# Multiplying dt u with B for two state steps in one VectorE instruction: a Mamba, GPTQ, attention and mixture sandwich on one core

## The chip, the cores and the metric

The kernel runs on one core of a Trainium2 chip. The metric is the device time of one execution in microseconds (us); three runs of the kernel before gave 953.85, 954.11 and 956.48, with a median of 954.11.

## The reference

Four layers, each `x = x + layernorm(layer(layernorm(x)))`, on x of 2 batches x 512 tokens x 512 channels, all in float32. The first layer is a Mamba block with 1024 inner channels and 16 states, the second a feed-forward layer with 4-bit weights that are unpacked first, the third an attention of one key head, the fourth a mixture of a shared feed-forward layer and a latent one. The change concerns the recurrence of the first, which runs over the tokens:

```python
def step(state, inp):
    dt_t, B_t, C_t, u_t = inp
    dA = jnp.exp(dt_t[..., None] * A)
    state = state * dA + (dt_t * u_t)[..., None] * B_t[:, None, :]
    y = jnp.einsum('bdn,bn->bd', state, C_t)
    return (state, y)
...
y = ys.transpose(1, 0, 2) + x * D
y = y * jax.nn.silu(gate)
return y @ W_out.T
```

## The kernel before

The inner channels lie on the 128 partitions, in 8 chunks, and the 512 tokens on the free axis. A "step" of the kernel is one batch, one chunk and two of the 16 states (NG = 2): 2 x 8 x 8 = 128 steps, numbered s; `k, gi = divmod(s, 8)` gives the chunk k (0 to 15, the second batch from 8 on) and the pair of states gi. In a step

- ScalarE makes exp(dt A) for both states into one of two PSUM tiles (`exps`, line 1002), two steps ahead;
- VectorE multiplies du (dt times u, 128x512, in PSUM, made once a chunk on line 1016) with B of the two states, broadcast over the partitions, into a state buffer `bx` of 128x1024 (`times_B`, line 1018), one step ahead;
- VectorE runs the recurrence over the tokens in place in `bx` (`scan`, line 1022);
- GpSimd multiplies `bx` with C, in place (`times_C`, line 1028); in some steps of the second batch it also adds the two states (line 1030);
- TensorE adds the two states (or their sum) into y in PSUM by matmuls with the identity (`sums`, line 1050), two steps later; the first of a chunk adds D u (line 1045). The gate is multiplied with y on VectorE (`fin`, line 1056) at gi = 2 of the next chunk.

`bx` comes from a pool of six buffers of one tag. A product that takes a buffer anew waits for the sums of the step that had it.

B and C are 16 tiles of 128x1024 (512 KB when written), one each for every gi. `states` loads them from a scratch in DRAM, broadcast to 128 partitions, on SP's DMA queue, B and C alternately: all 16 of the first batch just ahead of the loop, those of the second batch one gi a step during the last chunk of the first (steps 56 to 63).

In between, TensorE works through a fixed stream of other matmuls (`stream`: gates, the second batch's input projections, W_out of the first batch, and most of the second layer's first feed-forward product), portioned so that sums and stream together make 3.5 us a step by the kernel's own estimate (STEP). Other engines get the parts of these as jobs, released by a clock that ticks twice a step. The instruction order of TensorE, ScalarE, VectorE and GpSimd is that of the program's text: `pin` chains them. The order of SP's queue is the scheduler's. W_out's tiles (line 862) share three buffers with the other weights.

The main loop in its order, cut to what the change touches:

```python
for s in range(NS + 3):
    ...
    tick()
    if gi == 4 and k + 1 < len(order):
        diag(k + 1)
    if 0 < s < NS - 1:
        times_B(s + 1)
        if gi == NGI - 2 and k + 1 < len(order):
            new_du(k + 1)
    tick()
    if s < NS:
        scan(s)
```

`new_du` is ScalarE's copy of the next chunk's dt into du. So the order on VectorE is product, scan, product, scan, with jobs between.

Of the kernel before, what the change touches and what calls it, by code (L numbers as in the profile page):

```python
# [9 lines left out]
F32 = mybir.dt.float32  # L10
# [8 lines left out]
P = 128  # L19
B = 2  # L20
S = 512
# [13 lines left out]
NG = 2  # L35
NGI = N_ST // NG
# [20 lines left out]
def tile_sandwich(  # L57
# [72 lines left out]
    def minus_mean(mv, rs, name, n=TB, beside_scan=False):  # L130
        if beside_scan:
            nm = stat.tile([P, TB], F32, tag="nm", name=f"nm_{name}")
            if n == 1:
                nc.gpsimd.tensor_scalar(nm[:, :1], mv[:, 0, 0:1], rs[:, 0:1], -1.0, ALU.mult, ALU.mult)
            else:
                nc.gpsimd.tensor_mul(nm[:, :n], mv[:, :n, 0], rs[:, :n])
                nc.gpsimd.tensor_scalar(nm[:, :n], nm[:, :n], -1.0, None, ALU.mult)
            return nm
        nm = stat.tile([P, TB], F32, tag="nm", name=f"nm_{name}")
        nc.vector.scalar_tensor_tensor(  # L140
            nm[:, :n], mv[:, :n, 0], -1.0, rs[:, :n], ALU.mult, ALU.mult
        )
        return nm
# [278 lines left out]
    with ExitStack() as mamba:  # L422
# [3 lines left out]
        bcp = pool(mamba, "bc")  # L426
# [23 lines left out]
        for b in range(B):  # L450
            t_ = smp.tile([R_DT + 1, S], F32, tag=f"dtT{b}", name=f"dtT{b}")
# [3 lines left out]
        nc.gpsimd.dma_start(out=wx, in_=W_x)  # L455
        Bbs = [[None] * NGI for _ in range(B)]
        Cbs = [[None] * NGI for _ in range(B)]
        st = {}

        def w_in(part, b, c):  # L460
# [19 lines left out]
        def diag(k):  # L480

            c = k % NCH
            t_ = dgp.tile([P, P], F32, tag="dg", name=f"dg{k}")
            nc.scalar.activation(t_, ident, AF.Copy, scale=ch[:, c, KCONV + 1 : KCONV + 2])
            st["diag", k] = t_
# [49 lines left out]
        def states(b, gi):  # L535

            for lst, lo, nm in ((Bbs[b], 0, "B"), (Cbs[b], R_C - R_B, "C")):
                t_ = bcp.tile([P, NG, S], F32, tag=f"{nm}{gi}", name=f"{nm}{b}_{gi}")
                n0 = lo + gi * NG
                ins = nc.sync.dma_start(  # L540
                    out=t_, in_=scr[b][n0 : n0 + NG, :].partition_broadcast(P)
                )
                lst[gi] = t_
            return ins

        def dt_in(b, c):
            ps = mbank(f"pv{b}_{c}")
            nc.tensor.matmul(ps, wdt[:, ts(c, P)], dtT[b], start=True, stop=True)
            return ps
# [9 lines left out]
        with ExitStack() as p1:  # L559
# [10 lines left out]
            for i in range(TB + 2):  # L570
# [4 lines left out]
                if 0 <= i - 1 < TB:  # L575
                    j = i - 1
                    rs = rn[j]
                    nm = minus_mean(mvs[j], rs, f"m0_{j}", 1)
# [59 lines left out]
            for gi in range(NGI):  # L638
                last = states(0, gi)
# [8 lines left out]
            return g1p.tile([P, cols], dt, tag=f"g1{i}", name=name)  # L648

        with ExitStack() as p2:  # L650
            bxp = pool(p2, "bx", 6)
            ps_y = pool(p2, "p2y", 1, PSUM)
            ps_du = pool(p2, "p2du", 1, PSUM)
            ps_da1 = pool(p2, "p2da1", 1, PSUM)
# [13 lines left out]
            def spawn(gen, lag=0):  # L668
                jobs.append([now[0] + lag, gen])

            def tick():
                now[0] += 1
                for job in list(jobs):
                    if job[0] <= now[0]:
                        try:
                            job[0] = now[0] + next(job[1])
                        except StopIteration:
                            jobs.remove(job)
# [13 lines left out]
            def bank_free():  # L692
                return len(turns) < 2 or turns[-2][1] is not None
# [300 lines left out]
            NS = len(order) * NGI  # L994
            bxs = {}

            def exps(s):
                k, gi = divmod(s, NGI)
                b, c = order[k]
                for i in range(NG):  # L1000
                    n = gi * NG + i
                    nc.scalar.activation(  # L1002
                        das[s % 2][:, i, 1:], st["dt", b, c][:, 1:], AF.Exp, scale=A[:, c, n : n + 1]
                    )

            def new_du(k):

                b, c = order[k]
                du = st["du"] = ps_du.tile([P, S], F32, tag="du", name=f"du{b}_{c}")
                nc.scalar.copy(du, st["dt", b, c])  # L1010

            def times_B(s):
                k, gi = divmod(s, NGI)
                b, c = order[k]
                if gi == 0:
                    nc.vector.tensor_mul(st["du"], u[b][c], st["du"])
                bx = bxs[s] = bxp.tile([P, NG, S], F32, tag="bx", name=f"bx{b}_{c}_{gi}")
                nc.vector.tensor_mul(bx, st["du"].unsqueeze(1).to_broadcast([P, NG, S]), Bbs[b][gi])  # L1018

            def scan(s):  # L1020
                flat = bxs[s].rearrange("p n t -> p (n t)")
                nc.vector.tensor_tensor_scan(  # L1022
                    flat, das[s % 2].rearrange("p n t -> p (n t)"), flat, 0.0, ALU.mult, ALU.add
                )
# [7 lines left out]
            def paired(s):  # L1032

                k, gi = divmod(s, NGI)

                return order[k][0] == 1 and (k - NCH not in (2, 3) and gi in (1, 5) or k - NCH < 2 and gi % 2 == 1)

            def sums(s):
                k, gi = divmod(s, NGI)
                b, c = order[k]  # L1040
                ns = 1 if paired(s) else NG
                cost = ns * MM
                if gi == 0:
                    y = st["y"] = ps_y.tile([P, S], F32, tag="y", name=f"py{b}_{c}")
                    nc.tensor.matmul(y, st["diag", k], u[b][c], start=True, stop=False)
                    cost += MM
                bx = bxs.pop(s)
                for i in range(ns):
                    last = gi == NGI - 1 and i == ns - 1
                    nc.tensor.matmul(st["y"], ident, bx[:, i, :], start=False, stop=last)  # L1050
                return cost

            def fin(k):

                b, c = order[k]
                nc.vector.tensor_mul(g[b][c], g[b][c], st["y"])
                st[f"fin{k}"] = now[0]

            def dt_job(k, ps):
                dt_out(*order[k], ps)  # L1060
                release(f"pv{k}")
                yield 1
# [5 lines left out]
            exps(0)  # L1068
            exps(1)
            times_B(0)  # L1070
            free, dt_due = 0.0, None
            for s in range(NS + 3):
                k, gi = divmod(s, NGI)
                free = min(free, MM) + STEP
                if gi == 1 and k + 1 < len(order):
                    dt_due = k + 1
                if gi == 2 and k:
                    fin(k - 1)
                for part in ((1, 0) if gi == 2 or 2 <= s < NS + 2 and paired(s - 2) else (0, 1)):
                    if part == 0:  # L1080
                        if 0 <= s - 2 < NS:
                            free -= sums(s - 2)
                    else:
                        while free > 0 and s < NS:
                            if dt_due and bank_free():
                                turns.append([f"pv{dt_due}", None])
                                spawn(dt_job(dt_due, dt_in(*order[dt_due])), 2)
                                free -= MM
                                dt_due = None
                            cost = next(pe, None)  # L1090
                            if cost is None:
                                break
                            free -= cost
                tick()
                if gi == 4 and k + 1 < len(order):
                    diag(k + 1)
                if 0 < s < NS - 1:
                    times_B(s + 1)
                    if gi == NGI - 2 and k + 1 < len(order):
                        new_du(k + 1)  # L1100
                tick()
                if s < NS:
                    scan(s)
                    if s == 0:
                        times_B(1)
                    if s + 2 < NS:
                        exps(s + 2)
                    times_C(s)
                    if order[k] == (0, NCH - 1):
                        states(1, gi)  # L1110
                pin()
# [6 lines left out]
        with ExitStack() as p3:  # L1118
# [9 lines left out]
            for j in range(NCH // 2):  # L1128
                w = wo_pair(1, 0, j)
                for e in range(2):  # L1130
                    c = 2 * j + e
# [13 lines left out]
            for i, m in enumerate(IC):  # L1145
                j, e = divmod(i, 2)
                if not e:
                    w = wst.tile([P, 2, H], F32, tag="w4", name=f"wd0_{j}")
                    n = len(IC[i : i + 2])
# [287 lines left out]
```

## Time and profile before

| | |
|---|---|
| runs, median (lowest to highest) | 954.11 us (953.85 to 956.48) |
| the profiled execution, its own time | 955.89 us |
| its span, first to last instruction | 954.1 us |
| mean granted clock of TensorE | 0.959 |
| busy: TensorE, VectorE, GpSimd, ScalarE | 862.3, 675.2, 484.0, 420.2 us |
| first and last scan start | 74.0 and 570.4 us |

The profile is one execution. Its span is 1.8 us shorter than the time of the same execution, since that has what lies around the first and the last instruction. Busy time of TensorE is modelled, because matmuls overlap; its idle time before an instruction, with the engine that ended it, says more. In a group's line the two numbers after the bar are busy time in us and the mean duration of one in ns; after the second bar stands the idle time of the engine just before such instructions. In a timeline the first number is the start, the second the duration, in us; in brackets stand the idle time and what ended it. Durations on VectorE overlap with the next instruction's start, so what an instruction takes from the queue is read from start to start.

### The profile page before, as it was taken

Reading aid. Unit: us, or ns where it says so; the run is one execution under the profiler, and the core shown is the slowest. Engines: PE = TensorE matmul, PEld = TensorE weight load, DVE = VectorE, ACT = ScalarE, POOL = GpSimd, SP = SyncE. Lnnn points to the kernel's source line nnn. Section 1 sums busy time; section 2 is a strip of 40 time slices with the busy share of each in tenths; the row PEclk is TensorE's granted clock in tenths of the full one; section 3 lists DMA queues with packets and bytes.
Section 4 is the critical chain, followed back from the end, with each engine's and each line's share of the span. In section 5 each row is a group of like instructions: output and inputs, shape, how many; then the busy total and the mean of one; then the engine's idle time right before and its main releaser. Section 6 shows DMA issues by size and latency. Waiting matters only on the chain.

```text
span 954.1 us, 7148 instructions
## 1 busy us (share of the span) xinstructions
PE 862.3 (90%) x2184; PEld 386.6 (41%) x2184; DVE 675.2 (71%) x783; ACT 420.2 (44%) x631; POOL 484.0 (51%) x351
## 2 busy tenths in 40 slices
PE   6977989779989899579999999998999998999994
PEld 3532434333534434234433444444544444445441
DVE  4968999999999998999999995535610034534225
ACT  3335775656666655476655640125320014322122
POOL 5665796777877777876877884440000000011002
PEclk9978999898999989889999999999999999998997
DMA  6439211010002854300111103455223221200101
GB/s 182 163 124 387 69 37 38 30 37 31 22 23 83 297 187 152 89 0 0 45 44 45 30 9 124 150 159 198 58 64 89 58 89 45 66 12 30 48 0 44
DMA packets 43816, 80.08 MB, mean 84 GB/s; under 512 B 7774, under 2 KB 20937, under 8 KB 43778
## 3 DMA queue, kind: packets, MB, share of 16 engines
q1 hardware_dynamic: 41506, 73.64, 23.6%
q0 software_dynamic: 1984, 5.47, 1.6%
q10 hardware_dynamic: 288, 0.52, 0.2%
q8 instruction: 17, 0.28, 0.1%
q14 instruction: 21, 0.17, 0.1%
HBM read 68.37 MB, written 11.24 MB: 83 GB/s over the span
## 4 chain that ended last, share of the span: by engine, by line
PE 46%; DVE 28%; issue 11%; POOL 5%; DMA 2%; ACT 1%; SPq 0%; DVEq 0%; POOLq 0%; ACTq 0%
DVE bx L1022 11%; DVE bx L1018 8%; PE pd L1365 6%; PE py L1050 5%; PE pup L1302 5%; PE fo L1155 4%; PE fu L367 3%; PE fo L1218 3%; POOL bx L1028 3%; PE fg L367 3%; PE fu L947 3%; PE fg L947 3%; PE po L1133 3%; PE po L916 2%; DVE u L475 2%
## 5 line engine op out<-in xcount | busy, mean ns | idle before, releaser
L1028 POOL TENSOR_TENSOR bx<-bx,C 128x1024 f32<-128x1024 f32 x128 | 302.0, 2360 | 115.3 <-DVE bx L1022 90.7
L1022 DVE TENSOR_TENSOR_SCAN bx<-da,bx 128x1024 f32<-128x1024 f32 x128 | 291.6, 2279 | 0.1
L1050 PE MATMUL py<-bx,ident 128*128 128x512 f32 x480 | 238.1, 626 | 35.6 <-POOL bx L1028 32.3
L1002 ACT ACTIVATE da<-dt,A 128x511 f32<-128x511 f32 x256 | 176.3, 691 | 161.6 <-DVE bx L1022 155.7
L1018 DVE TENSOR_TENSOR bx<-du,B 128x1024 f32<-128x1024 f32 x128 | 154.4, 1206 | 9.0 <-DMA B<-scr 5.1
L1050 PEld LDWEIGHTS py<-bx,ident 128*128 128x128 f32 x480 | 91.5, 198 | 164.1 <-issue 93.1
L1231 DVE TENSOR_TENSOR it<-it,fu 128x512 f32<-128x512 f32 (+1 forms) x11 | 7.6, 688 | 72.3 <-PE fu L367 72.3
L1302 PE MATMUL pup<-hT_l,wup 128*128 128x512 f32 x128 | 57.5, 604 | 0.0
L381 POOL TENSOR_TENSOR sd<-ve,half 128x4 f16<-128x4 f16 x2 | 2.1, 1045 | 109.0 <-DVE ve L379 109.0
L709 PE MATMUL pg<-xT,w_g 128*128 128x512 f32 x120 | 57.1, 604 | 0.0
L1365 PE MATMUL pd<-wdn,hid 128*128 128x512 f32 x128 | 55.3, 592 | 0.0
L127 POOL TENSOR_TENSOR rs_lo<-ve_lo,mhalf 128x1 f32<-128x1 f32 x8 | 5.5, 684 | 78.0 <-DVE ve_lo L125 78.0
L947 PE MATMUL fg<-hT_f,wg 128*128 128x512 f32 (+1 forms) x88 | 42.1, 597 | 0.0
L475 DVE SCALAR_TENSOR_TENSOR u<-px,ch,u 128x511 f32<-128x511 f32 (+2 forms) x48 | 35.8, 746 | 7.0 <-ACT u L468 5.9
L367 PE MATMUL fg<-hT_f,wg 128*128 128x512 f32 (+1 forms) x88 | 40.2, 593 | 0.7 <-ACT hT_f L171 0.7
L947 PE MATMUL fu<-hT_f,wu 128*128 128x512 f32 (+1 forms) x88 | 40.7, 592 | 0.0
L367 PE MATMUL fu<-hT_f,wu 128*128 128x512 f32 (+1 forms) x88 | 39.8, 593 | 0.0
L1218 PE MATMUL fo<-wd,it 128*128 128x512 f32 (+1 forms) x88 | 39.6, 592 | 0.0
L1155 PE MATMUL fo<-wd,it 128*128 128x512 f32 (+1 forms) x88 | 38.0, 593 | 1.6 <-DMA wd<-wd_d 1.6
L1365 PEld LDWEIGHTS pd<-wdn,hid 128*128 128x128 f32 x128 | 24.2, 190 | 30.7 <-issue 30.1
L1302 PEld LDWEIGHTS pup<-hT_l,wup 128*128 128x128 f32 x128 | 24.5, 195 | 28.8 <-issue 28.8
L1230 ACT ACTIVATE it<-fg 128x512 f32<-128x512 f32 (+1 forms) x11 | 6.6, 597 | 65.7 <-PE fg L367 65.7
(224 smaller groups left out, 1161.4 us busy)
## 6 DMA issues: line engine op xcount, KB each, us to landing
wo<-in_W_outT SPq DMA_DIRECT2D x20, 512.0 KB
B<-scr SPq DMA_DIRECT2D x16, 512.0 KB
C<-scr SPq DMA_DIRECT2D x16, 512.0 KB
wg<-wgu_d SPq DMA_DIRECT2D x10, 512.0 KB
wu<-wgu_d SPq DMA_DIRECT2D x10, 512.0 KB
w_x<-in_W_in SPq DMA_DIRECT2D x8, 512.0 KB
wgu_d<-w_gu POOLq DMA_DIRECT2D x16, 256.0 KB, 2.3
w_g<-in_W_in SPq DMA_DIRECT2D x8, 512.0 KB
```

What stands on the lines that cost most here:

```text
L367: nc.tensor.matmul(ps[:m], w[:, kc, e * P : e * P + m], hT[:, kc, :], start=(kc == 0), stop=(kc == KH - 1),)
L709: nc.tensor.matmul(ps, w[:, k, ts(e, P)], xT[b][:, k, :], start=(k == 0), stop=(k == KH - 1))
L947: nc.tensor.matmul(ps[:m], wt[j][a][:, kc, e * P : e * P + m], hT[:, kc, :], start=(kc == 0), stop=(kc == KH - 1),)
L1002: nc.scalar.activation(das[s % 2][:, i, 1:], st["dt", b, c][:, 1:], AF.Exp, scale=A[:, c, n : n + 1])
L1018: nc.vector.tensor_mul(bx, st["du"].unsqueeze(1).to_broadcast([P, NG, S]), Bbs[b][gi])
L1022: nc.vector.tensor_tensor_scan(flat, das[s % 2].rearrange("p n t -> p (n t)"), flat, 0.0, ALU.mult, ALU.add)
L1028: nc.gpsimd.tensor_mul(bxs[s], bxs[s], Cbs[b][s % NGI])
L1050: nc.tensor.matmul(st["y"], ident, bx[:, i, :], start=False, stop=last)
L1155: nc.tensor.matmul(fo[t], its[i][:m, ts(t, P)], w[:m, e], start=(i == 0), stop=(i == len(IC) - 1),)
L1218: nc.tensor.matmul(fo[t], its[i][:m, ts(t, P)], w[:m], start=(i == 0), stop=(i == len(IC) - 1),)
L1302: nc.tensor.matmul(ps, w[:, kc, ts(e, P)], src[kc], start=(kc == 0), stop=(kc == KH - 1))
L1365: nc.tensor.matmul(pd, hid[kc][:, ts(i, P)], wdn[kc], start=(kc == 0), stop=(kc == INT // P - 1),)
```

## The change

VectorE multiplies du with B for two steps at once, 128x2048 in place of 128x1024. For that, B's tiles of gi and gi + 1 are halves of one tile, and so are the state buffers of steps s and s + 1; the pool has three such pairs in place of six single buffers. The product is issued in every odd step, ahead of that step's scan, for the two steps that follow. The products of steps 0 and 1 stay single, each into its half of the first pair. Scans, products with C, sums, loads and all other instructions keep their sizes.

```diff
@@ states @@
             for lst, lo, nm in ((Bbs[b], 0, "B"), (Cbs[b], R_C - R_B, "C")):
-                t_ = bcp.tile([P, NG, S], F32, tag=f"{nm}{gi}", name=f"{nm}{b}_{gi}")
+                if nm == "B":
+                    if gi % 2 == 0:
+                        two = bcp.tile([P, 2 * NG, S], F32, tag=f"B{gi}", name=f"B{b}_{gi}")
+                        B2s[b][gi // 2] = two
+                    t_ = B2s[b][gi // 2][:, gi % 2 * NG : (gi % 2 + 1) * NG, :]
+                else:
+                    t_ = bcp.tile([P, NG, S], F32, tag=f"{nm}{gi}", name=f"{nm}{b}_{gi}")
                 n0 = lo + gi * NG
...
-            bxp = pool(p2, "bx", 6)
+            bxp = pool(p2, "bx", 3)
@@ times_B @@
                 if gi == 0:
                     nc.vector.tensor_mul(st["du"], u[b][c], st["du"])
-                bx = bxs[s] = bxp.tile([P, NG, S], F32, tag="bx", name=f"bx{b}_{c}_{gi}")
-                nc.vector.tensor_mul(bx, st["du"].unsqueeze(1).to_broadcast([P, NG, S]), Bbs[b][gi])
+                def product(dst, by):
+                    n = dst.shape[1]
+                    nc.vector.tensor_mul(dst, st["du"].unsqueeze(1).to_broadcast([P, n, S]), by)
+
+                if s % 2 == 0:
+                    two = bxp.tile([P, 2 * NG, S], F32, tag="bx", name=f"bx{b}_{c}_{gi}")
+                    for i in range(2):
+                        bxs[s + i] = two[:, i * NG : (i + 1) * NG, :]
+
+                if s > 1:
+                    product(two, B2s[b][gi // 2])
+                else:
+                    product(bxs[s], Bbs[b][gi])
@@ the main loop @@
+                if s % 2 and s < NS - 1:
+                    times_B(s + 1)
                 if 0 < s < NS - 1:
-                    times_B(s + 1)
                     if gi == NGI - 2 and k + 1 < len(order):
                         new_du(k + 1)
```

More of the change, by code (lines that the diff above doesn't have):

```diff
@@ L457, in tile_sandwich @@
         Cbs = [[None] * NGI for _ in range(B)]
+        B2s = [[None] * (NGI // 2) for _ in range(B)]
         st = {}
```

## The prediction

> **What bounds the kernel now.** I read the page's table of slices first (who is full, and where), then the costliest groups, then busy time in hand-chosen windows, then timelines of VectorE and TensorE.
>
> ```profile
> PE   6977989779989899579999999998999998999994
> DVE  4968999999999998999999995535610034534225
> ```
>
> In the two rows of tenths the scan stage is slices 4 to 24 (about 74 to 577 us), and VectorE and TensorE are both near full there. After it VectorE drops to 3 to 5 tenths and TensorE stays at 9, so VectorE can only matter inside the scan stage. The windows cut that stage where the bound changes (TensorE, weight loads, VectorE, ScalarE and GpSimd busy, each with a count, then clock, DMA share, GB/s):
>
> ```profile
> 80.00:331.00 251.00, 221.96 (x546) 97.17 (x544) 246.25 (x189) 163.14 (x251) 191.87 (x107) 0.95 0.24 83
> 331.00:371.00 40.00, 38.43 (x77) 15.67 (x78) 34.44 (x28) 22.53 (x31) 31.73 (x20) 0.87 0.57 192
> 371.00:430.00 59.00, 42.70 (x96) 17.22 (x94) 56.52 (x52) 33.53 (x47) 45.91 (x34) 0.88 0.19 60
> 430.00:477.00 47.00, 46.45 (x107) 19.89 (x108) 45.36 (x31) 29.86 (x44) 35.72 (x18) 1.00 0.08 23
> 477.00:577.00 100.00, 97.00 (x222) 40.50 (x220) 96.05 (x66) 53.43 (x82) 81.05 (x42) 1.00 0.13 36
> ```
>
> From 80 to 331 and from 371 to 430 VectorE is full (246.25 of 251) and TensorE has holes: VectorE sets the pace. From 331 to 371 and 430 to 477 it is TensorE. From 477 to 577 both are full within 4%. The two instructions concerned, and GpSimd's product behind them:
>
> ```profile
> L1028 POOL TENSOR_TENSOR bx<-bx,C 128x1024 f32<-128x1024 f32 x128 | 302.0, 2360 | 115.3 <-DVE bx L1022 90.7
> L1022 DVE TENSOR_TENSOR_SCAN bx<-da,bx 128x1024 f32<-128x1024 f32 x128 | 291.6, 2279 | 0.1
> L1018 DVE TENSOR_TENSOR bx<-du,B 128x1024 f32<-128x1024 f32 x128 | 154.4, 1206 | 9.0 <-DMA B<-scr 5.1
> ```
>
> The means, 1206 and 2279 ns, are not what an instruction costs the queue. The VectorE timeline shows starts (first column) closer together than durations (second):
>
> ```profile
> 72.64 1.22 DVE L1018 TENSOR_TENSOR bx<-du,B 128x1024 f32<-128x1024 f32 x1 [3.74 <-DMA B<-scr]
> 73.97 2.29 DVE L1022 TENSOR_TENSOR_SCAN bx<-da,bx 128x1024 f32<-128x1024 f32 x1
> 76.34 1.23 DVE L1018 TENSOR_TENSOR bx<-du,B 128x1024 f32<-128x1024 f32 x1
> 78.89 1.23 DVE L1018 TENSOR_TENSOR bx<-du,B 128x1024 f32<-128x1024 f32 x1 [1.32 <-DMA B<-scr]
> 80.03 2.28 DVE L1022 TENSOR_TENSOR_SCAN bx<-da,bx 128x1024 f32<-128x1024 f32 x1
> 82.22 1.20 DVE L1018 TENSOR_TENSOR bx<-du,B 128x1024 f32<-128x1024 f32 x1
> 83.34 2.28 DVE L1022 TENSOR_TENSOR_SCAN bx<-da,bx 128x1024 f32<-128x1024 f32 x1
> ```
>
> Product to scan is 83.34 - 82.22 = 1.12 us, scan to product 82.22 - 80.03 = 2.19. Further on a 128x512 product of the same engine starts at 113.10 and the next instruction at 113.68: 0.58. TensorE's waits in the scan stage:
>
> ```profile
> PE py L1050 <- POOL bx L1028: 31.6, 27, 4.1
> PE py L1045 <- DVE g L1056: 14.0, 5, 4.8
> PE po L916 <- DMA wo<-in_W_outT: 0.9, 1, 0.9
> ```
>
> 27 times it waits for a step's product with C (31.6 us). Its own timeline places these: many before 331 and from 371 to 430, none from 432 to 490, then six short ones (0.85, 0.30, 0.34, 0.28, 0.44 and 0.79 us, at 490, 505, 519, 534, 563 and 577).
>
> [...] The trace has half-clock stretches (granted clock 0.50 from 86 to 90, after a 4.05 us idle at 84.79); I can't say where they fall next time.
>
> **The change part by part**, against the profiled span of 954.1 us (the execution's own time is 955.89, the median of three runs 954.11; a difference found on the span is laid on the median).
>
> *Fewer instructions.* Steps 0 and 1 stay single; steps 2 to 127 become 63 products of 128x2048. [...] All 63 give 3.2 us. Only those where VectorE is the bound count: 32 pairs up to 331 (-1.6), 7 from 371 to 430 (-0.4), and after 477 twelve more, -0.6. Elsewhere TensorE hides them. That a scan follows a scan costs nothing extra: the last two of before do so, and start 2.19 us apart (568.21 and 570.40).
>
> *A wait added at the start.* The product for steps 2 and 3 needs B of step 3 too and stands on VectorE's queue ahead of scan 1. B and C come alternately, 512 KB each, and the DMA engines are full (413 to 422 GB/s from 74 to 90 us), so 1.25 us per tile; B of step 3 comes two tiles after B of step 2, whose wait ended at 78.9. So 81.3: +2.5 us, less the saving of two pairs, +2.4 by step 4. Queued behind it are scan 1 and all of VectorE. The next pair starts at about 87.9 and its B lands at about 86.3: no second wait. VectorE has no idle from 80 to 216 in which to lose this, so it is paid in full. TensorE is 3.5 late there (scan 1 comes after the whole double product); it has 4.4 us of waits between 126 and 138 to catch up.
>
> *The order of work.* VectorE's order becomes pair, scan, scan, pair, scan, scan. A scan of an odd step is now one product (1.1 us) later against the work done, that of an even step is where it was. Where the lead passes from VectorE to TensorE at an odd step this costs 1.1: step 63 at 331.66 and step 87 at 430.55. Where it passes back it gives 1.1: at 370.84 VectorE waits 3.42 us for y of the chunk before, and one product more is done by then; likewise at the end, step 127. Costs and gains: +1.1, -1.1, +1.1, -1.1. A state buffer half is free of false waits: in the built order the second half's scan waits for ScalarE alone.
>
> *Three pairs in place of six.* A pair's buffer is taken anew by the product ordered three pairs on, and needs the sums of both its steps. In the trace the sums of steps 65 and 67 end at 349.81 and 356.68, the products that would take their place start at 348.19 and 356.45. So VectorE waits up to 1.7 us longer there. It is hidden: TensorE is the bound until 371, and VectorE waits 3.42 at its end anyhow. At the other pairs the sums are done 1 us or more ahead (least at step 89: 444.09 against 445.07).
>
> *du.* ScalarE's copy of dt into du no longer waits for the last product, which is now a step earlier: nothing, since du is waited for 0.7 us in all before.
>
> *B's pairs and SP's queue.* SP's order in the built program differs in one thing that counts: the first W_out tile (wo) is issued before C of step 4 of the second batch, not behind C of step 7. Before, TensorE waited 0.91 us for it at 337.65, because SP held it until the product of step 63 with C had ended. It now lands some 10 us earlier, and the second tile is needed two matmuls later: -0.9. C of step 4 isn't needed for 25 us.
>
> *Sum.* 2.4 - 1.6 + 1.1 - 0.9 = +1.0 at TensorE's stage from 331; -1.1 - 0.4 = -0.5 at 430; +1.1 = +0.6 through TensorE's stage to 477; -0.6 in the six short holes after it, and GpSimd's last products (570.99 and 574.52, behind another of its jobs) keep the last -1.1 from showing. Net 0.0: **954.1 us**.
>
> **Rivals.**
>
> *Faster by the durations (0.10).* If a double product took its mean's worth off the queue[...]: 39 pairs where VectorE is the bound give 5.4, the holes after 477 give 2.2 in place of 0.6, start and order as above: 954.1 + 2.4 - 0.9 - 5.4 - 2.2 = 948.0. The starts speak against it.
>
> *Faster by the clock (0.20).* The half-clock stretch at 332 to 342 lies on TensorE's path from 337.65 on, 5 us at half speed. With the 0.91 wait gone and other idle stretches, it may fall elsewhere: -2.5, and with the start's wait partly lost in TensorE's holes -1: 950.6.
>
> *Slower by clumps (0.26).* Sums now reach TensorE in twos, with longer idle between. If that brings one more half-clock stretch of 6.8 us to the stage from 430 to 577, where TensorE has 3.0 us of holes in all, 3.4 us of matmul time is lost on the path: 957.5. [...] for it: clock 0.74 to 0.91 where TensorE waits much (380 to 420). Against: from 430 on the clock is 1.00 throughout.
>
> *It doesn't do what it says.* No chance: the built order of VectorE has two single and 63 double products.
>
> **How the numbers follow.** The forecast has 0.44. About 0.3% (2.9 us) is what a measurement here tells from no change. Faster by that 0.30 (the two faster rivals), within it 0.44, slower 0.26. The likeliest's own range is 952 to 956.5: [...] a start of one tile (1.2) or of 2.9 in place of 2.4 takes 1.2 off or adds 0.5. For 8 in 10: 950.0 to 958.0.
>
> **What would show it.** The 63 double products last 2.27 us and start 2.19 before the next instruction; the wait for B near 79 is about 3.8 in place of 1.32; TensorE's wait at 84.79 becomes 7.5; its wait for wo is gone; the six holes after 477 shrink. It is wrong if the double product starts are much under 2.1 us apart from what follows, if products wait for sums outside 340 to 360, or if the clock of 430 to 577 falls under 1.00.

## The result: 0.6% slower, and the profile after

Six runs of after, with six of before on the same chip: 961.3 us (959.15 to 962.52) against 954.78 (953.83 to 956.48). The ratio is 1.0059, with a 95% interval of 1.0039 to 1.0078: some 5.6 us slower, outside the range of 950 to 958. The profiled execution of after took 962.52 (span 960.7), that of before 955.89 (954.1), a pair of much the same distance (6.6). Of all runs told of below one was slower at a lower clock (975.12 us at 0.950, in e12), and it is left out of that kernel's time and ratio; with it the median is 962.9, as an expectation has it.

First the table of slices and the costliest groups of after; then its windows, in the same stretches as before's (busy time of TensorE, weight loads, VectorE, ScalarE and GpSimd with counts, then clock, DMA share, GB/s).

```profile
PE   6966979797999989689999999999999998999994
DVE  4958998999998999999999994545510024525225
...
L1040 DVE TENSOR_TENSOR_SCAN bx<-da,bx 128x1024 f32<-128x1024 f32 x128 | 288.3, 2274 | 1.0 <-ACT da L1009 0.9
L1068 PE MATMUL py<-bx,ident 128*128 128x512 f32 x480 | 239.4, 630 | 41.8 <-POOL bx L1046 37.0
...
L1026 DVE TENSOR_TENSOR bx<-du,B 128x2048 f32<-128x2048 f32 (+1 forms) x65 | 145.5, 2239 | 12.9 <-DMA B<-scr 7.6
```

```profile
80.00:331.00 251.00, 219.38 (x535) 96.52 (x534) 241.12 (x153) 159.25 (x247) 187.33 (x105) 0.93 0.21 76
331.00:371.00 40.00, 36.61 (x80) 14.90 (x78) 38.08 (x25) 21.41 (x32) 30.34 (x18) 0.96 0.63 216
371.00:430.00 59.00, 45.19 (x99) 18.28 (x99) 55.12 (x46) 36.09 (x50) 49.89 (x37) 0.89 0.23 71
430.00:477.00 47.00, 44.46 (x100) 18.78 (x99) 44.88 (x26) 28.84 (x42) 32.89 (x16) 0.95 0.08 23
477.00:577.00 100.00, 97.45 (x223) 41.17 (x222) 97.05 (x55) 56.41 (x87) 79.08 (x41) 1.00 0.11 30
```

VectorE's products took 145.5 us in place of 154.4, yet its busy time from 80 to 331 fell by 5 us in a stage that it bounds: 251 less 241 is 10 us of idle, where before had 5. TensorE's waits for GpSimd grew from 32.3 to 37.0 (the sums' group) and the clock of 430 to 477 fell from 1.00 to 0.95.

Where the difference came is seen by setting each instruction of after beside its own in before, step by step (start after less start before, us):

| place | scan | sums | what happened there in after |
|---|---|---|---|
| step 4 | +2.1 | +3.1 | the double product waits 3.83 for B, scan 1 stands behind it |
| step 14 | +1.9 | +2.7 | 0.05 a pair saved |
| step 15, last of its chunk | +3.8 | +3.7 | du waited for, scan behind a double product |
| step 16 | +2.7 | +8.0 | half clock on TensorE (granted 0.50 from 140.8 to 154.5) |
| step 63, last of its chunk | +7.4 | +7.3 | VectorE had waited 3.60 for u at 156 |
| step 75 | +4.1 | +4.1 | TensorE's stage: no wait for the first wo tile, less half clock |
| step 86 | +2.1 | +2.1 | VectorE's stage gives 2.0 back |
| step 87, last of its chunk | +4.2 | +4.1 | du waited for, scan behind a double product |
| step 88 | +3.1 | +5.7 | half clock on TensorE (0.50 from 434.4 to 437.8) |
| gate of the last chunk (`fin`) | +6.6 | | scans wait 0.45 for da at 508 and 537, the sums of step 127 wait 1.46 in place of 0.79 |

An odd step's scan is 1.1 late in this order everywhere (+3.0 at step 13, +1.9 at 14), so a step is best set beside one of its kind. From step 13 to 15 the scan loses 0.8 and from 85 (+3.2) to 87 1.0, about what VectorE waits for du there. The sums lose 1.0 at each of the two, and by the next step 4.2 and 1.5 more. Whether the 1.1 or du counts, this trace alone doesn't tell; the experiments do.

The losses come in jumps, at ends of chunks: steps 15 to 16, and 87 to 88. VectorE's timeline of before at the first, and then of after at both:

```profile
130.96 0.68 DVE L1016 TENSOR_TENSOR du<-u,du 128x512 f32<-128x512 f32 x1
131.77 1.23 DVE L1018 TENSOR_TENSOR bx<-du,B 128x1024 f32<-128x1024 f32 x1
132.91 2.28 DVE L1022 TENSOR_TENSOR_SCAN bx<-da,bx 128x1024 f32<-128x1024 f32 x1
```

```profile
127.98 4.45 DVE L1040 TENSOR_TENSOR_SCAN bx<-da,bx 128x1024 f32<-128x1024 f32 x2
132.36 0.53 DVE L233 TENSOR_SCALAR q_gu<-qw_gu 128x352 int32<-128x352 int32 x1
133.67 0.70 DVE L1023 TENSOR_TENSOR du<-u,du 128x512 f32<-128x512 f32 x1 [0.79 <-ACT du L1017]
134.50 2.29 DVE L1026 TENSOR_TENSOR bx<-du,B 128x2048 f32<-128x2048 f32 x1
136.71 4.46 DVE L1040 TENSOR_TENSOR_SCAN bx<-da,bx 128x1024 f32<-128x1024 f32 x2
...
156.24 2.32 DVE L476 SCALAR_TENSOR_TENSOR u<-px,ch,u 128x511 f32<-128x511 f32 x3 [3.60 <-ACT u L469]
...
426.89 0.69 DVE L1023 TENSOR_TENSOR du<-u,du 128x512 f32<-128x512 f32 x1 [0.97 <-ACT du L1017]
```

At a chunk's end three things stand ahead of its last scan: the next chunk's du (0.83 from start to start), which has to wait for ScalarE, and the first product, now 2.2 long in place of 1.1. The scan of step 15 is the one at 132.91 in before, and in after the first of the two in the row at 136.71. TensorE's timeline of before, and then of after, at the same sums:

```profile
137.75 3.68 PE L1050 MATMUL py<-bx,ident 128*128 128x512 f32 x4 [2.02 <-POOL bx L1028]
141.35 1.12 PE L548 MATMUL pv<-dtT,wdt 33*128 33x512 f32 x2
142.41 0.66 PE L784 MATMUL tp_n<-ident,xn_n 128*128 128x128 f32 x4
143.74 5.42 PE L709 MATMUL px<-xT,w_x 128*128 128x512 f32 x12 [0.67 <-ACT xT L787]
...
426.44 1.98 PE L1050 MATMUL py<-bx,ident 128*128 128x512 f32 x4 [1.33 <-POOL bx L1028]
428.26 0.60 PE L784 MATMUL tp_f<-ident,xn_f 128*128 128x128 f32 x4
430.55 1.98 PE L1050 MATMUL py<-bx,ident 128*128 128x512 f32 x4 [1.70 <-POOL bx L1028]
```

```profile
141.47 3.78 PE L1068 MATMUL py<-bx,ident 128*128 128x512 f32 x4 [3.08 <-POOL bx L1046]
145.18 2.07 PE L555 MATMUL pv<-dtT,wdt 33*128 33x512 f32 x2
147.18 1.11 PE L791 MATMUL tp_n<-ident,xn_n 128*128 128x128 f32 x4
148.97 8.14 PE L716 MATMUL px<-xT,w_x 128*128 128x512 f32 x12 [0.68 <-ACT xT L794]
...
426.22 5.49 PE L1068 MATMUL py<-bx,ident 128*128 128x512 f32 x8 [2.31 <-POOL bx L1046]
431.55 0.60 PE L791 MATMUL tp_f<-ident,xn_f 128*128 128x128 f32 x4
434.69 3.51 PE L1068 MATMUL py<-bx,ident 128*128 128x512 f32 x4 [2.54 <-POOL bx L1046]
```

TensorE waits 3.08 in place of 2.02, and 2.54 in place of 1.70. What follows is dearer than the wait: in before the granted clock is 0.50 from 137.9 to 141.3 and back at 1.00 after the four sums; in after it is 0.50 from 140.8 to 154.5, and the stream's next matmuls (pv, tp and most of px) run at half clock too (2.07 against 1.12, 8.14 against 5.42 for the same matmuls). At 434.69 the four sums take 3.51 where before's took 1.98. px then reaches ScalarE late, which makes u from it, and that is VectorE's wait of 3.60 for u at 156.24.

### The profile page after: what moved, and what is told of

The parts are those of the page before. It is cut to its first block, busy times and chain, and to the rows that moved or that the text cites. A ratio compares the mean times of both kernels' runs of the same rounds, so it can differ in the third digit from the quotient of the medians.

```text
span 960.7 us, 6964 instructions
## 1 busy us (share of the span) xinstructions
PE 865.2 (90%) x2184; PEld 387.8 (40%) x2184; DVE 674.6 (70%) x720; ACT 419.8 (44%) x631; POOL 483.8 (50%) x351
## 4 chain that ended last, share of the span: by engine, by line
PE 41%; DVE 14%; POOL 4%; ACT 3%; issue 2%; DMA 1%; POOLq 0%; SPq 0%; DVEq 0%; ACTq 0%
DVE bx L1040 6%; PE pd L1384 6%; PE pup L1321 5%; PE fo L1174 4%; PE fg L367 4%; PE py L1068 4%; PE fu L367 4%; DVE bx L1026 3%; PE fo L1237 3%; PE po L1152 3%; POOL bx L1046 2%; PE po L923 2%; PE fu L954 1%; PE pr L1352 1%; PE fg L954 1%
## 5 line engine op out<-in xcount | busy, mean ns | idle before, releaser
L1040 DVE TENSOR_TENSOR_SCAN bx<-da,bx 128x1024 f32<-128x1024 f32 x128 | 288.3, 2274 | 1.0 <-ACT da L1009 0.9
L1026 DVE TENSOR_TENSOR bx<-du,B 128x2048 f32<-128x2048 f32 (+1 forms) x65 | 145.5, 2239 | 12.9 <-DMA B<-scr 7.6
L1237 PE MATMUL fo<-wd,it 128*128 128x512 f32 (+1 forms) x88 | 39.6, 592 | 0.0
```

Of the source, the lines that this page charges most:

```text
L1026: nc.vector.tensor_mul(dst, st["du"].unsqueeze(1).to_broadcast([P, n, S]), by)
L1040: nc.vector.tensor_tensor_scan(flat, das[s % 2].rearrange("p n t -> p (n t)"), flat, 0.0, ALU.mult, ALU.add)
L1237: nc.tensor.matmul(fo[t], its[i][:m, ts(t, P)], w[:m], start=(i == 0), stop=(i == len(IC) - 1),)
```

## The experiments

Sixteen kernels ran, in four groups; before ran with every group, with medians of 954.75 to 955.75 over 36 to 51 runs. The time is the median. Ratios are to before in the same group, and can differ by some 0.1% from those of the medians. The two columns on the right come from the one profiled execution of each, which can lie 5 or 6 us from the median (e3 and e7 below it, e16 above): TensorE's idle time ahead of the sums of the last step of a chunk (7, 15, ... 127), added over the 16 chunks, and the time at half clock (granted 0.50) between 74 us and the gate of the last chunk, worked out as twice the mean loss of granted clock times the length.

| run | time | ratio, 95% | waits at chunk ends | half clock |
|---|---|---|---|---|
| before | 954.8 | | 10.9 | 48 |
| after | 961.3 | 1.0059 [1.0039, 1.0078] | 18.3 | 55 |
| e1 scan 1 first | 961.4 | 1.0049 [1.0030, 1.0068] | 21.6 | 44 |
| e2 two single products | 959.7 | 1.0054 [1.0032, 1.0076] | 21.1 | 41 |
| e3 pair tiles, old order | 956.6 | 0.9999 [0.9979, 1.0019] | 12.2 | 38 |
| e5 before, wo early | 953.6 | 0.9970 [0.9955, 0.9985] | 13.5 | 34 |
| e7 du early | 959.2 | 1.0042 [1.0020, 1.0064] | 16.0 | 44 |
| e8 du early, scan 1 first | 957.8 | 1.0037 [1.0014, 1.0060] | 19.5 | 55 |
| e9 du early, ends single | 953.6 | 0.9984 [0.9965, 1.0003] | 8.0 | 38 |
| e10 before, wo early, du late | 989.6 | 1.0366 [1.0326, 1.0407] | 39.6 | 61 |
| e11 ends single | 959.1 | 1.0043 [1.0026, 1.0060] | 11.7 | 58 |
| e12 late at the ends only | 962.4 | 1.0077 [1.0049, 1.0105] | 25.7 | 34 |
| e13 ends single at three | 955.8 | 1.0001 [0.9979, 1.0022] | 13.3 | 41 |
| e14 e9 with scan 1 first | 951.4 | 0.9960 [0.9947, 0.9973] | 10.2 | 34 |
| e15 e14 with single products | 953.7 | 0.9972 [0.9956, 0.9988] | 10.4 | 38 |
| e16 e12 with wo early | 963.3 | 1.0092 [1.0057, 1.0127] | 27.1 | 41 |
| e17 e11 with wo early | 957.9 | 1.0015 [0.9995, 1.0034] | 8.8 | 51 |
| e18 e14, two wo tiles early | 950.5 | 0.9933 [0.9906, 0.9959] | 10.2 | 34 |

### Taking the parts of the change apart (e1, e2, e3, e5)

e1 puts scan 1 ahead of the first double product:

```diff
-                if s % 2 and s < NS - 1:
+                if s % 2 and 1 < s < NS - 1:
                     times_B(s + 1)
...
-                    if s == 0:
-                        times_B(1)
+                    if s < 2:
+                        times_B(s + 1)
```

> The changed kernel with one swap: scan 1 goes ahead of the double product of steps 2 and 3. Start theory (the product's wait for B of step 3 holds scan 1, TensorE starts its sums 3.1 us late and loses more at half clock later): scan 1 starts near 77.3 us, TensorE's wait at its second sum falls from 7.5 us to about 2, and the time falls from the changed kernel's 961.3 by 3 to 6 us, to 955 to 958. Order theory (odd scans come a product later all through the stage): at most 2.5 us less, 959 or more.

e2 keeps after's order, and makes each double product two of 128x1024 in the same place:

```diff
-                    product(two, B2s[b][gi // 2])
+                    for i in range(2):
+                        product(bxs[s + i], Bbs[b][gi + i])
```

> The changed kernel with each double product issued as two of 128x1024 in the same place. Order and start are those of the changed kernel, only the merging is gone. If the loss is from order and start: as slow as the changed kernel or 1 to 3 us slower, 961 to 965 (63 times 0.05 us of issue time). If the double instruction itself is what hurts: faster than the changed kernel, 958 or less.

e3 keeps after's pairs of tiles and its three pairs of buffers, with single products in before's order:

```diff
-                if s > 1:
-                    product(two, B2s[b][gi // 2])
-                else:
-                    product(bxs[s], Bbs[b][gi])
+                product(bxs[s], Bbs[b][gi])
...
-                if s % 2 and s < NS - 1:
-                    times_B(s + 1)
                 if 0 < s < NS - 1:
+                    times_B(s + 1)
```

> The kernel before with B's tiles and the state buffers in pairs (three pairs), and products single and in their old order. Buffer theory (a pair is freed only when both halves are summed): 2 us or more slower than before. Order and start theories: within 1 us of before, 954 to 956.

e5 is before with one thing changed: the first wo tile is asked for early, so that SP issues it in the place that it has in after, ahead of C of step 4:

```diff
+                st["wo"] = wo_pair(0, 0, 0)
                 for a in range(KH // 2):
                     ps = yield from bank(f"pfe{a}")
...
-                ws = {}
+                ws = {0: st["wo"]}
```

> The kernel before with the first W_out tile asked for earlier, so that its load stands on SP's queue where it stands in the changed kernel, ahead of C of step 4 of the second batch; nothing else differs. If the earlier load explains what the changed kernel wins back around 340 us: 0.9 to 3.3 us faster than before, 951.5 to 954. If that gain was the clock's: no change, 954.5 to 955.5.

The pairs of tiles and buffers cost nothing that can be measured (e3), and the product's longer wait for its buffer (3.06, where before waits 1.94) is there and hidden. This line of e3's VectorE timeline shows it; TensorE sets the pace at that place (busy for 36.53 of 40 us from 331 to 371 in e3):

```profile
347.57 1.22 DVE L1026 TENSOR_TENSOR bx<-du,B 128x1024 f32<-128x1024 f32 x1 [3.06 <-PE py L1065]
```

Whether a pair is one instruction or two makes no difference that can be told in after's order (e2). The start can't be the loss by itself (e1): VectorE was level with before at step 14 there, and then waited 2.06 for du at 133. The early wo tile is worth 0.3% in before (e5), and after has the tile as early, and falls back by 3.2 us less at that place (sums +7.3 at step 63, +4.1 at 64). If that gain is after's too, the rest of the change loses not 0.6% but the distance from e5 to after, 7.7 us by the medians. The two theories left are du and the late scans.

### du or the last scan (e7 to e10)

In after, `new_du` at gi = 6 orders ScalarE's copy behind the exponentials of the chunk's last step, which need the scan two steps before, an odd one. e7 orders it a step earlier, just behind the product for steps 6 and 7:

```diff
-                    if gi == NGI - 2 and k + 1 < len(order):
+                    if gi == NGI - 3 and k + 1 < len(order):
                         new_du(k + 1)
```

> After's order of VectorE, but ScalarE's copy of dt into du for the next chunk is ordered one step earlier (right behind the product for steps 6 and 7 of a chunk, ahead of the exponentials of step 7, not behind them). Du theory (the copy stands behind exponentials that wait for the late odd scan, and this delay starts the losses at steps 15 and 87): VectorE's waits for du near 133 and 427 (0.79 and 0.97 in after) fall under 0.2 us, the sums of step 87 wait under 2.0 us in place of 2.54, the half-clock stretches between 427 and 438 are gone, and the time is 957 to 959. Order theory (odd scans one product late by themselves make TensorE wait in longer pieces): du waits go, but the half-clock stretches near 141 to 154 and 428 to 438 stay and the time is 960 to 962.

e8 is e7 with e1's edit.

> As the run with the early copy of du, and scan 1 stands ahead of the first double product as well. If start and du make up the loss between them: 953.5 to 956. If the order of odd scans is the cause by itself: 959 to 962, as with scan 1 first alone (961.4).

e9 is e7 with the first two products of every chunk single and in the old order:

```diff
-                if s > 1:
+                if gi > 1:
                     product(two, B2s[b][gi // 2])
...
-                if s % 2 and s < NS - 1:
+                if (s % 2 or gi == 0 and s) and s < NS - 1:
                     times_B(s + 1)
```

> The early copy of du, and the first two products of every chunk are single and in the old order (product, scan, product, scan), so the last scan of a chunk is not one product late; 48 double products stay. Order theory at the chunk ends: the sums of steps 15, 63 and 87 come 1.1 us earlier than with the early copy alone, no half-clock stretch between 427 and 438, 955 to 958. Du theory: as with the early copy alone, within 1 us. If odd scans late inside the chunk count (steps 1, 3, 5), it stays at 959 to 962.

e10 is e5 with du's copy put behind the next chunk's first exponentials, a dose of late du and nothing else of the change:

```diff
-                    if gi == NGI - 2 and k + 1 < len(order):
-                        new_du(k + 1)
...
                         exps(s + 2)
+                    if s and gi == NGI - 2 and k + 1 < len(order):
+                        new_du(k + 1)
                     times_C(s)
```

> The order and the single products of before, with the first wo tile asked for early (953.6 without further change), and ScalarE's copy of du put behind the next exponentials: a dose of du's lateness with no other part of the change. Du theory: VectorE waits for du over 0.5 us at several of the chunks' first products, and the time rises by 2 to 5, to 955.5 to 958.5. Order theory: the waits are there and get lost in slack, 953 to 955.

e7 took the waits for du away (none over 0.2 us in the loop) and gained 2 us by the medians, with overlapping intervals; its 22 runs scatter from 952.8 to 965.2, and its profile is of the fastest. So du isn't the whole. With the last scan of a chunk no longer late as well (e9), the loss is gone. e8 shows why the start alone helped little: with TensorE no longer behind, it waits 2.15 us at the end of the first chunk, and a half-clock stretch follows, as in e1.

e10 missed by far: 36 us more than e5, where 2 to 5 were expected. The copy stands behind exponentials that wait for scan 6 of the chunk, after which VectorE has nothing but du's product. Its timeline:

```profile
170.27 2.28 DVE L1023 TENSOR_TENSOR_SCAN bx<-da,bx 128x1024 f32<-128x1024 f32 x1
174.54 0.70 DVE L1017 TENSOR_TENSOR du<-u,du 128x512 f32<-128x512 f32 x1 [1.99 <-ACT du L1011]
```

All 15 ends of chunks ahead of another have such a wait, 1.99 at eleven of them, 31.9 us together, and the gate of the last chunk is 34.1 later than in e5: in the sum, what VectorE waited at the chunks' ends was not made good later.

### The size of each (e11 to e14, e16, e17)

e11 is after with e9's single products at the ends, and du's copy where after has it.

> After, and the first two products of every chunk single and in the old order; ScalarE's copy of du stays where after has it. The same with an early copy of du ran in 953.6, the early copy alone in 959.2. Chunk-end theory (the last scan of a chunk, one product late, is what costs): 953 to 956, du waits of up to 1 us or not. Du theory (both are needed, the late copy alone costs 2 us or more): 956.5 to 959.

e12 is the other way round: before's order, and only the products for steps 0 and 1 of a chunk are one double product, ahead of the last scan of the chunk before:

```diff
-                if s > 1:
+                if k and gi < 2:
                     product(two, B2s[b][gi // 2])
...
-                if s % 2 and s < NS - 1:
+                if 0 < s < NS - 1 and (gi or k == 0):
                     times_B(s + 1)
```

> The order of before and single products (with after's pair tiles and early wo tile), but for one thing: the products for steps 0 and 1 of a chunk are one double product ahead of the last scan of the chunk before, so that one scan in eight is a product late. Chunk-end theory: 957.5 to 961, near after. Theory that late odd scans inside the chunks, or the sum of many, cost: 953 to 956, near the order of before with wo early (953.6).

e13 is e9 with single products at three chunk ends only, those of steps 15, 63 and 87:

```diff
-                if gi > 1:
+                if gi > 1 or k not in (0, 2, 8, 11):
                     product(two, B2s[b][gi // 2])
...
-                if (s % 2 or gi == 0 and s) and s < NS - 1:
+                if (s % 2 or gi == 0 and k in (2, 8, 11)) and s < NS - 1:
                     times_B(s + 1)
```

> Early copy of du, and single products in the old order only at the three chunk ends where the lead passes to TensorE or its long wait stands (steps 15, 63 and 87). Handoff theory: all of the gain of doing so at every chunk end, 953 to 956. If every chunk end costs a little: 957 to 960, near the early copy of du alone (959.2).

e14 is e9 with e1's edit.

> Early copy of du, single products at every chunk end, and scan 1 ahead of the first double product: every part of after that costs taken away, 47 or 48 double products kept. If the start's 2.4 us are paid and the saved issue cost is real (24 double products where VectorE is the bound, some 1.2 us): 950 to 952.5, better than before with wo early (953.6). If the start's wait is lost in TensorE's waits as the run with scan 1 first alone suggests: 953 to 954.5.

In the built order of e12 the first wo tile stood behind C of step 7, unlike what its expectation says, and in e11 too. e16 and e17 are these two with e5's edit, and are the ones to go by.

> Late at the chunk ends only (962.9 with wo late), now with the first wo tile early. If lateness at the chunk ends alone costs what the whole change loses beside wo: 958 to 961. If the late wo tile made up most of its loss: 953.5 to 956.

> Single products at the chunk ends with the late copy of du (959.1 with wo late), now with the first wo tile early. If the late copy of du costs by itself (waits of 1.13 and 1.22 us at 133 and 425, and what follows them): 956 to 958.5. If wo made the difference to the run with early du (953.6): 953 to 955.

One scan in eight a product late, and nothing else of the change, makes the kernel 0.9% slower than before (e16), 9.8 us above e5 by the medians: at least all that the change lost. How a wait of 1 us grows is seen in the first two chunks of e16. TensorE's timeline:

```profile
108.16 2.47 PE L1069 MATMUL py<-bx,ident 128*128 128x512 f32 x4 [2.16 <-POOL bx L1047]
110.56 2.07 PE L555 MATMUL pv<-dtT,wdt 33*128 33x512 f32 x2
112.56 4.71 PE L716 MATMUL pg<-xT,w_g 128*128 128x512 f32 x6
...
140.96 3.78 PE L1069 MATMUL py<-bx,ident 128*128 128x512 f32 x4 [6.07 <-POOL bx L1047]
144.67 2.07 PE L555 MATMUL pv<-dtT,wdt 33*128 33x512 f32 x2
```

Its ScalarE timeline between the two:

```profile
128.53 0.60 ACT L689 ACTIVATE th<-pg 128x512 f32<-128x512 f32 x1 [4.13 <-PE pg L716]
...
132.56 0.57 ACT L1018 COPY du<-dt 128x512 f32<-128x512 f32 x1
```

And its VectorE timeline:

```profile
133.17 0.70 DVE L1024 TENSOR_TENSOR du<-u,du 128x512 f32<-128x512 f32 x1 [3.58 <-ACT du L1018]
```

In e5 the sums of step 7 wait 1.25 and pv and pg then run at full clock (1.12 and 2.84). In e16 they wait 2.16, and pv and pg take 2.07 and 4.71. The gate's matmuls are late, so ScalarE's tanh waits 4.13 for them. Behind the tanh in ScalarE's queue stands the copy of du, VectorE waits 3.58 for that, and TensorE's sums of step 15 wait 6.07 for what stands behind VectorE's late scan: the wait has gone round all three engines and come back greater. This is how one execution of e16 lost (968.55 us, 5.2 above the median), and not the whole of it. e12's profile, with the same order up to there, has no half clock at 108 and waits 0.36 for du, and its sums still fall back beside e3's, which has the same tiles and the old order: from +0.5 at step 16 to +2.2 at 55, +4.6 at 87 and +5.8 at 127, mostly by 0.5 to 1.1 at a chunk's end. In the last stage, from 477 to 577, e16's granted clock is 1.00, and it still falls back by 1.1 us at each of steps 103 and 111 (its sums less e5's go from 13.00 to 14.08 and from 13.52 to 14.60), and has half of that back after the first.

With the ends free, the late copy seems to cost something by itself: e17 against e9 is 1.0015 against 0.9984, 0.3% with intervals that overlap a little, so at the edge of the noise. Freeing three ends (e13) gives most of what all 15 give (e9); the two are not told apart. e14 is faster than before by 0.4%. TensorE's timeline of e14, at the ends of the first two chunks and of the eleventh:

```profile
108.09 1.98 PE L1068 MATMUL py<-bx,ident 128*128 128x512 f32 x4 [1.07 <-POOL bx L1046]
110.00 1.12 PE L555 MATMUL pv<-dtT,wdt 33*128 33x512 f32 x2
...
136.87 1.98 PE L1068 MATMUL py<-bx,ident 128*128 128x512 f32 x4 [1.14 <-POOL bx L1046]
138.78 1.12 PE L555 MATMUL pv<-dtT,wdt 33*128 33x512 f32 x2
...
423.05 1.98 PE L1068 MATMUL py<-bx,ident 128*128 128x512 f32 x4 [1.59 <-POOL bx L1046]
```

Waits of 1.07, 1.14 and 1.59, where e1 had 2.15 at the first and after 3.08 and 2.54 at the others. Four sums take 1.98 each time and pv behind the first two 1.12, as at full clock in before. (px, further behind, still meets half clock in e14 too, from 142 to 146: its twelve matmuls take 7.11 there, 5.42 in before.)

### What merging is worth, and the second wo tile (e15, e18)

e15 is e14 with e2's edit.

> As the run with early du, single products at the chunk ends and scan 1 first (951.4), but every double product is two of 128x1024 again, in the same place. If the saved issue cost is real on the path (24 or so pairs where VectorE is the bound, 0.05 each, and some of those after 477): 952.5 to 953.5. If merging is worth nothing: 951 to 952.

e18 is e14 with the first two wo tiles asked for where e5 asks for the first:

```diff
+                st["wo"] = [wo_pair(0, 0, j) for j in range(2)]
...
-                ws = {}
+                ws = dict(enumerate(st["wo"]))
```

> As the run with early du, single products at the chunk ends and scan 1 first (951.4), with the second wo tile asked for ahead of C of step 6 as well. If TensorE's wait of 2.4 us for it at 337 is on the path: 949 to 950.5. If the stage's holes take it up: 951 to 952.5.

e15 is 0.12% of before's time behind e14, 2.2 us by the medians, and the intervals overlap: in line with 48 times the 0.05 us that a double product's start to start saves (2.4 us), not shown. e18 has the lowest time of all, 0.9933 [0.9906, 0.9959], with six runs; against e14 it isn't told apart either. Both e14 and e18 are faster than before and than after. But they have the early wo tile, as after has, and e5, which merges nothing, has 0.9970 by that alone: e14 isn't told apart from e5. So the runs show that the loss can be taken away with 48 merges kept, and not that the merges gain anything.

## Why the prediction was wrong

*Fewer instructions*: right in size. The 3.2 us for 63 pairs, 0.05 each, were an estimate of mine; the starts of before give 0.04 (two products of 128x512 at 0.58 less one of 128x1024 at 1.12). Double products last 2.26 to 2.29 and start 2.17 to 2.21 ahead of what follows where nothing is waited for, and VectorE's distance to before falls from 2.14 to 1.86 over six pairs, 0.05 each. (The working counts the first two pairs twice, 0.1 us.) What that is worth at the end only e14 and e15 come near to showing. VectorE was full up to 331 in before (246.25 of 251 us), and still after is at 1.0059, while e9 and e14, which keep 48 of the 63 merges and have the ends single and du early, are at 0.9984 and 0.9960: what stands behind the larger instruction counted for more than the 0.05.

*A wait added at the start*: right in size (3.83 on VectorE, 7.56 on TensorE, against 3.8 and 7.5), wrong in its consequence. TensorE was to catch up in its waits of 126 to 138, and it did not: its lateness made ScalarE's work late, and so the copy of du. The start may be paid once nothing else hides it: e14 against e9, 0.9960 against 0.9984, is 2.3 us, but the intervals overlap. In after itself taking it away gained nothing (e1), as TensorE then waited at the end of the first chunk instead.

*The order of work*: **the step that failed.** It charged the product's 1.1 us at two handoffs, steps 63 and 87, and gave it back at 371 and at the end; the other ends of chunks, and all that follows a longer wait of TensorE, it put at nothing. A chunk's end is a handoff in its own right. There du's product and the next chunk's first product stand ahead of the last scan on VectorE, and TensorE waits for that scan's sums in nine chunks of before, for 10.9 us in all. The trace of before had shown this: the waits at 137.75, 331.66 and 430.55, and three of the six "short holes", those at 490, 519 and 577, are all at a last step. After waits 18.3 there (though 3.9 less than before at the steps just ahead of them), and e12 and e16, with nothing but this lateness, lose 0.8 and 0.9% (e3 and e5, their like without it, lose nothing). In after's trace the end at step 15, charged nothing, takes 5.3 us between the sums of steps 14 and 16. The give-back after 371 did come (sums +4.1 at step 75, +2.1 at step 86); the next chunk end, charged 1.1, took 2.0 at step 87 and 3.6 by step 88.

*Three pairs in place of six*: right in the main. The waits of 1.56 at 353.98 in after and of 3.06 in e3 are hidden by TensorE's stage, and e3 is at 0.9999. But a product also waits 1.71 for sums at 449.85, outside the stretch of 340 to 360, where the forecast saw 1 us to spare: with TensorE 5.7 late from step 88 on and the scans only 3 to 4, the spare was gone. TensorE's sums stay at +5.7 there, so this too is hidden.

*du*: **failed too.** (The 0.7 us in the working is what products wait for du's product; for the copy itself VectorE waits nowhere in before's loop.) That the copy no longer waits for the last product is true, and doesn't count: it stands in ScalarE's queue behind the exponentials of the last step, which wait for an odd scan, now late, and behind whatever TensorE makes late. It was waited for 0.79 and 0.97 us in after. e17 against e9 puts it at 0.3%, at the edge of the noise; in e10 the loss was about what was waited (34.1 for 31.9).

*B's pairs and SP's queue*: right in sign, too small. The early wo tile is worth 2.9 us in before (0.9970, so 1.4 to 4.3), not 0.9. Part of the difference may be half clock, 34 us against 48 in the profiled runs, which are one execution each. With the ends late it gains nothing that shows (e16 against e12).

*The rivals.* "Slower by clumps", at 957.5, had the right side and part of the mechanism: the half-clock stretches at 427 to 431 and 434 to 438 (granted 0.50) are in after, and one in that place in e1 and e2, none in before, e3 and e5. After's first follows a wait of TensorE of 2.31 us that ended at 426.22, and its second sets in at 434.38, near the end of one of 2.54. But I put these waits down to sums in twos anywhere. Twos do lengthen a wait: the one of 2.31 stands ahead of the sums of steps 85 and 86, where before has two of 1.33. e9 has the same wait (2.30 at 420.25) with half clock behind it. Yet the runs with double products inside the chunks and single ones at the ends (e9 at 0.9984, e14 at 0.9960) have no loss against before, so it is the chunk's last scan that decides, not the twos.

How much of the loss is the clock and how much the waits themselves isn't settled. At step 87 of after the waits add 2.0 us and the half clock 1.5. Over the span, though, e12 and e16 lose the most but for e10, with no more half clock than others, and a stretch in one profile need not be in the next run.

"Faster by the durations" took 5.4 us for 39 pairs, 0.14 each. That is what the durations did lose (2.27 in place of 2 x 1.206), and the starts lost 0.05.

## What to carry to other kernels

Where each group of steps ends in something that the next group waits for (an accumulation closed, a factor made anew), a larger instruction ahead of the last step of the group can cost more than merging saves, as here (e16, with 15 such instructions, is 9.8 us above e5; 63 merges at 0.05 are 3.2): find in the profile which step of a group the bound engine waits for before choosing where to merge. When an instruction moves by a microsecond, follow what waits for it through every in-order queue, the third engine's too; here a scan late by one product came back through ScalarE's copy of du, as a wait of 3.58 us on VectorE in e16. Keep two single instructions at the group's end and merge the rest: e14 kept 48 of 63 merges and lost nothing, though a gain from them isn't shown.

## What the runs showed of the hardware

In the traces of before and after the records of the granted clock hold 0.50 and 1.00 alone. Time at half clock came in units of 3.4 us in all 18 profiles (34.1, 37.5, 41.0, ... 61.4 us), and a wait of 2.15 us was followed by it (e1 and e8 at 108 to 110), while one of 2.70 at 426 in e7 was not. The records tell the two apart: in each trace every change lies on one grid of 3.41 us, so the idle time can be counted by stretches of that grid. In the 18 traces, from 74 to 570 us, TensorE was at full clock in 2367 stretches. Where it was idle for 2.0 us or more of one (by its modelled ends), the next was at half clock in 105 of 105; under 1.0 us in none of 2029; between, in 27 of 233. Before and after alone have 13 of 13, none of 224 and 2 of 22. Stretches of e1, and then of e7, show it (TensorE's busy time stands behind the length of the stretch, the granted clock third from the right):

```profile
106.67:110.08 3.41, 1.26 (x4) 0.38 (x3) 3.41 (x5) 2.76 (x5) 2.75 (x2) 1.00 0.45 154
110.08:113.50 3.42, 3.42 (x5) 1.05 (x4) 3.42 (x2) 2.69 (x4) 3.25 (x4) 0.50 0.00 0
```

```profile
421.56:424.97 3.41, 2.07 (x8) 0.88 (x6) 3.41 (x3) 1.05 (x2) 1.04 (x1) 1.00 0.00 0
424.97:428.38 3.41, 2.05 (x5) 0.82 (x6) 3.41 (x3) 3.11 (x5) 3.41 (x2) 1.00 0.00 0
428.38:431.80 3.42, 3.42 (x8) 1.40 (x9) 3.42 (x3) 2.77 (x4) 1.53 (x2) 1.00 0.00 0
```

The grid falls across e7's wait of 2.70 and leaves 1.3 us of it on either side, and the clock stays at 1.00; e1's wait of 2.15 lies in one stretch, and the next is at 0.50. Of these two waits the shorter cost clock and the longer did not.

Runs of one and the same program differ in their clock: the 22 runs of e7 had a granted clock of 0.953 to 0.968 and took 952.8 to 965.2 us, with a correlation of -0.78 between the two and 0.8 us for each 0.001. The standard deviation of the times was 4.3 us for e7 and 1.7 for e14, also of 22 runs. One profile of a kernel is thus a poor witness of its clock: that of e7 fell on its fastest run.
